# Moving delta*u*B of 14 of 16 states to GpSimd in the last image, with the scan tiled by one state

## The chip, the cores and the metric

The kernel runs on one core of one Trainium2 chip. The metric is the device time of one execution in microseconds (us). The kernel before was run three times: 26,690.43, 26,701.57 and 26,703.51 us, so the median is 26,701.57 us. One more execution was taken with the hardware profiler; all views below come from that one.

## The reference, cut to what matters

The input x holds 4 images of 128 x 128 positions with 128 channels, in fp32. Layer 0 is a group norm, a deformable 3x3 convolution (offsets, a bilinear gather, a depthwise and a pointwise convolution) and a residual sum. Layer 1 takes the result, norms it, and runs two Mamba blocks over it, each image row being one sequence of 128 steps. The part that the change touches is the selective scan of such a block:

```python
def _selective_scan(u, delta, A, Bm, Cm, Dp):
    deltaA = jnp.exp(jnp.einsum('btd,dn->btdn', delta, A))
    deltaBu = jnp.einsum('btd,btn->btdn', delta * u, Bm)
    ...
    def step(h, xs):
        dA, dBu, c = xs
        h = dA * h + dBu
        y = jnp.einsum('bdn,bn->bd', h, c)
        return (h, y)
    ...
    return y + u * Dp
```

There are d = 256 inner channels and n = 16 states. For each state the kernel needs the decay exp(delta*A), the product delta*u*B, the recurrence h = decay*h + product along the 128 steps, the product h*C, and the sum of that over the 16 states.

## The kernel before, in words

**Layer 0** goes image by image, through `layer0(b)`. Its costliest parts are `gather` (L364: GpSimd issues four indirect DMAs per half unit, 9,216 in all) and `sample` (L382: VectorE weights the gathered values, then TensorE sums and transposes them at L128 through `add_transposed`).

**Layer 1** goes by blocks of 4 rows (SR = 4), which is 512 positions (TB = 512) on the free axis, with channels on the 128 partitions, in two halves (NC = 2). There are 32 blocks per image and 128 in all. A job is one block through one of the two Mamba blocks, so there are 64 jobs per image and 256 in all. `pre(st, l)` makes u, the gate g, delta (tile `de`), delta*u (tile `du`), and a DRAM tile `bcd` with the rows of B and C. `main(st, l)` runs the scan in pairs of states (NQ = 2), 8 pairs per job, 2,048 pairs in all. For each pair:

- SyncE issues two DMAs that spread two rows of B (tile `bc0`) and two rows of C (tile `bc1`) over 128 partitions (L570), each with two buffers.
- ScalarE first writes zeros over the first step of each sequence in the decay tile `da` (L575), since the scan runs on through sequence after sequence and a decay of zero starts a new one. Then it writes the other 127 steps of the decays with four exponentials (L580). There are three `da` tiles of two states each.
- VectorE makes delta*u*B into `hs`, one instruction per state (L586). `hs` has one buffer of two states.
- VectorE scans both states in one instruction of 2,048 elements (L592). It writes over the decays in `da`.
- VectorE multiplies both states by C in one instruction, in place in `da` (L596).
- TensorE adds the transposed products into `y` in PSUM, 16 matmuls of 128x128 (L128).

L586 and L596 are written as `scalar_tensor_tensor` with `ones[:, 0:1]` as a scalar read from memory, where a plain `tensor_tensor` would compute the same.

```python
df = da.rearrange("p c n s t -> p (c n s t)")
nc.vector.tensor_tensor_scan(
    df, df, hs.rearrange("p c n t -> p (c n t)"), zero[:, 0:1], ALU.mult, ALU.add
)
```

After the last pair VectorE multiplies y by the gate (L607), TensorE transposes it and projects it; at the second Mamba block ScalarE copies the result to `ot` (L630), and SyncE writes it out (L632).

**What sets the order.** The two layers overlap by one image: the loop at the end of `block_kernel` steps through layer 0 of image b + 1 and layer 1 of image b in turn. So image 0's layer 0 runs alone, then three stretches have both, and layer 1 of the last image (image 3) runs alone. `pre` of the next job is written down ahead of `main` of the present one. Within this the framework's scheduler orders the instructions of each engine[...].

Of the kernel before, what the change touches and what calls it, by code (L numbers as in the profile page):

```python
# [10 lines left out]
F32 = mybir.dt.float32  # L11
I32 = mybir.dt.int32
AF = mybir.ActivationFunctionType
ALU = mybir.AluOpType
# [3 lines left out]
P = 128  # L18
G = 2
CG = 64  # L20
NT = 9
RB = 8
SR = 4
TB = SR * P
NGT = 4
NL = 2
NC = 2
NS = 16
NQ = 2
DTR = 8  # L30
DCONV = 4
# [32 lines left out]
def block_kernel(ctx: ExitStack, tc: tile.TileContext, a: dict, out: bass.AP):  # L64
    nc = tc.nc
    x = a["x"]
    B, H, W, C = x.shape
# [21 lines left out]
    cw = ctx.enter_context(tc.tile_pool(name="w", bufs=1))  # L89
# [4 lines left out]
    p2 = ctx.enter_context(tc.tile_pool(name="l1p2", bufs=1))  # L94
# [4 lines left out]
    def loadw(name, shape, src=None, pool=cw, tag=None):  # L99
        t = pool.tile(shape, F32, name=f"w_{name}", tag=tag) if tag else pool.tile(shape, F32, name=f"w_{name}")  # L100
        nc.sync.dma_start(t, a[name] if src is None else src)
        return t
# [13 lines left out]
    ones = cw.tile([P, P], F32, name="ones")  # L116
# [5 lines left out]
    inc = cw.tile([P, NL, DCONV, NC * P], F32, name="inc")  # L122
    aneg = cw.tile([P, NL, NC, NS], F32, name="aneg")
    ddiag = cw.tile([P, NL, NC, P], F32, name="ddiag")

    def add_transposed(o, v, start, stop):

        nc.tensor.matmul(o, v, ident, is_transpose=True, start=start, stop=stop, skip_group_check=True)  # L128
# [4 lines left out]


    dw = loadw("dw", [P, NT, NT], pool=p2, tag="dbl")
    dwb = loadw("dwb", [P, NT], pool=p2, tag="ot")
    pw = loadw("pw", [P, NT, CG], pool=p2, tag="u")
    pwb = loadw("pwb", [P, 1], pool=p2, tag="w1")
    nc.vector.tensor_tensor(
# [15 lines left out]
    alog = loadw("alog", [P, NL, NC, NS], pool=p2, tag="dbl")  # L155
    nc.scalar.activation(aneg, alog, AF.Exp)
    nc.vector.tensor_scalar(aneg, aneg, -1.0, None, ALU.mult)
    dpar = loadw("dpar", [P, NL, NC], pool=p2, tag="ot")
    for l in range(NL):
        for c in range(NC):  # L160
            nc.vector.tensor_scalar(ddiag[:, l, c, :], ident, dpar[:, l, c : c + 1], None, ALU.mult)
    inw = loadw("inw", [P, NL, NC * P], a["inw"][:, :, 0 : NC * P], pool=p2, tag="yg")
    cvw = loadw("cvw", [P, NL, DCONV, NC * P], pool=p2, tag="hs")
    for l in range(NL):
        nc.vector.tensor_tensor(
            inc[:, l], cvw[:, l], inw[:, l].unsqueeze(1).to_broadcast([P, DCONV, NC * P]), ALU.mult
        )


# [289 lines left out]

    NDA = 3
    das = [cw.tile([P, NC, NQ, SR, P], F32, name=f"da{i}") for i in range(NDA)]
    zero = cw.tile([P, NC * NQ * SR], F32, name="zero")
    nc.vector.memset(zero, 0.0)
    n_da = [0]

    NH = 2
# [5 lines left out]
    def next_h():  # L474
        n_h[0] += 1
        return hps[n_h[0] % NH]

    def load_x1(blk, nm):
        b, off = divmod(blk * TB, H * W)
        t = p2.tile([P, TB], F32, tag="x1t", name=f"x1t_{nm}", bufs=2)  # L480
        nc.sync.dma_start(t, x1[b][:, off : off + TB])
        return t
# [70 lines left out]
    def main(st, l):  # L553

        blk = st["blk"]
        nm = f"{blk}_{l}"

        y = psy.tile([P, SR, NC, P], F32, tag="y", name=f"y_{nm}")
        for i in range(SR):
            for c in range(NC):  # L560
                nc.tensor.matmul(  # L561
                    y[:, i, c], st["u"][:, c, i * P : (i + 1) * P], ddiag[:, l, c, :],
                    start=(i % 2 == 0 and c == 0), stop=False, skip_group_check=True,
                )
        for q in range(NS // NQ):
            bc = []
            for w in range(2):
                t = p2.tile([P, NQ, TB], F32, tag=f"bc{w}", name=f"bc{w}_{nm}_{q}", bufs=2)
                n0 = w * NS + q * NQ
                nc.sync.dma_start(t, st["bcd"][n0 : n0 + NQ, :].partition_broadcast(P))  # L570
                bc.append(t)
            da = das[n_da[0] % NDA]
            n_da[0] += 1

            nc.scalar.copy(da.rearrange("p c n s t -> p (c n s) t")[:, :, 0], zero)  # L575
            for c in range(NC):
                dv = st["delta"][:, c].rearrange("p (s t) -> p s t", s=SR)
                for n in range(NQ):
                    s = q * NQ + n
                    nc.scalar.activation(  # L580
                        da[:, c, n, :, 1:], dv[:, :, 1:], AF.Exp, scale=aneg[:, l, c, s : s + 1]
                    )
            hs = p2.tile([P, NC, NQ, TB], F32, tag="hs", name=f"hs_{nm}_{q}")

            for n in range(NQ):
                nc.vector.scalar_tensor_tensor(  # L586
                    hs[:, :, n, :], st["du"], ones[:, 0:1],
                    bc[0][:, n].unsqueeze(1).to_broadcast([P, NC, TB]),
                    op0=ALU.mult, op1=ALU.mult,
                )  # L590
            df = da.rearrange("p c n s t -> p (c n s t)")
            nc.vector.tensor_tensor_scan(  # L592
                df, df, hs.rearrange("p c n t -> p (c n t)"), zero[:, 0:1], ALU.mult, ALU.add
            )
            dc = da.rearrange("p c n s t -> p c (n s t)")
            nc.vector.scalar_tensor_tensor(  # L596
                dc, dc, ones[:, 0:1],
                bc[1].rearrange("p n t -> p (n t)").unsqueeze(1).to_broadcast([P, NC, NQ * TB]),
                op0=ALU.mult, op1=ALU.mult,
            )  # L600
            for c in range(NC):
                for n in range(NQ):
                    for i in range(SR):
                        add_transposed(y[:, i, c], da[:, c, n, i, :], False, q == NS // NQ - 1 and n == NQ - 1)
            yield
        gt = st["g"]
        nc.vector.tensor_tensor(gt, y.rearrange("p s c d -> p s (c d)"), gt, ALU.mult)  # L607
        yg = p2.tile([P, NC, TB], F32, tag="yg", name=f"yg_{nm}")
        for c in range(NC):
            pt = ps1.tile([P, SR, P], F32, tag="t", name=f"pyg_{nm}_{c}")  # L610
            for i in range(SR):
                nc.tensor.transpose(pt[:, i, :], gt[:, i, c * P : (c + 1) * P], ident)  # L612
            nc.scalar.copy(yg[:, c], pt.rearrange("p s t -> p (s t)"))
        po = ps1.tile([P, TB], F32, tag="t", name=f"pout_{nm}")
        if l < NL - 1:
            for c in range(NC):
                nc.tensor.matmul(po, ow[:, l, c, :], yg[:, c], start=(c == 0), stop=(c == NC - 1))
            st["h"] = next_h()
            nc.scalar.copy(st["h"][:, :, DCONV - 1 :], po.rearrange("p (s t) -> p s t", s=SR))
        else:  # L620
            x1t = load_x1(blk, f"o{nm}")
            for i in range(SR):
                o = po[:, i * P : (i + 1) * P]
                nc.tensor.matmul(o, x1t[:, i * P : (i + 1) * P], ident, start=True, stop=False)
                for c in range(NC):
                    nc.tensor.matmul(
                        o, yg[:, c, i * P : (i + 1) * P], ow[:, l, c, :], start=False, stop=(c == NC - 1)
                    )
            ot = p2.tile([P, SR, P], F32, tag="ot", name=f"ot_{nm}")
            nc.scalar.copy(ot.rearrange("p r c -> p (r c)"), po)  # L630
            b, row = divmod(blk * SR, H)
            nc.sync.dma_start(out[b, row : row + SR].rearrange("r w c -> w r c"), ot)  # L632
# [8 lines left out]
    def layer1():  # L641
        pre(*jobs[0])
        for i, job in enumerate(jobs):
            if i + 1 < len(jobs):
                pre(*jobs[i + 1])
            yield from main(*job)
# [11 lines left out]
    n0 = NJ * NT  # L658
# [67 lines left out]
def build(arrays):  # L726

    import concourse.bacc as bacc

    nc = bacc.Bacc("TRN2", target_bir_lowering=False, num_devices=1)  # L730
    a = {
        k: nc.dram_tensor(f"in_{k}", v.shape, mybir.dt.from_np(v.dtype), kind="ExternalInput").ap()
        for k, v in arrays.items()
    }
    out = nc.dram_tensor("out_0", arrays["x"].shape, F32, kind="ExternalOutput").ap()
    with tile.TileContext(nc) as tc:
        block_kernel(tc, a, out)
    return nc
# [9 lines left out]
```

## Time and profile before

| what | value |
|---|---|
| median of three runs | 26,701.57 us |
| the profiled execution's own time | 26,698.06 us |
| span of the profiled execution, first to last instruction | 26,696.0 us |
| VectorE (DVE) busy | 23,505.8 us, 88% |
| TensorE (PE) busy | 19,620.5 us, 73% |
| GpSimd (POOL) busy | 16,017.0 us, 60%; the last gather starts at 21,045.0 us |
| ScalarE (ACT) busy | 11,605.1 us, 43% |
| DMA | 143 GB/s on average |

The profile's first part gives the busy time of each engine. Its second part cuts the span into 40 equal slices of 667 us and gives the busy share of each slice in tenths, so a 9 is 90% or more. Its fifth part lists groups of like instructions with their count, their busy time, the mean duration of one in nanoseconds, and the idle time of the engine just before them, with what ended it. In a timeline a line is one instruction or a run of like ones: its start, its length, the engine, the line of the kernel, and what it writes and reads. Durations of neighbours on VectorE overlap a little (one starts some 0.08 us before the one ahead of it is over), so what an instruction costs is read from one start to the next.

### The profile page before, as it was taken

Reading aid. Unit: us, or ns where it says so; the run is one execution under the profiler, and the core shown is the slowest. Engines: PE = TensorE matmul, PEld = TensorE weight load, DVE = VectorE, ACT = ScalarE, POOL = GpSimd, SP = SyncE. Lnnn points to the kernel's source line nnn. Section 1 sums busy time; section 2 is a strip of 40 time slices with the busy share of each in tenths; the row PEclk is TensorE's granted clock in tenths of the full one; section 3 lists DMA queues with packets and bytes.
Section 4 is the critical chain, followed back from the end, with each engine's and each line's share of the span. In section 5 each row is a group of like instructions: output and inputs, shape, how many; then the busy total and the mean of one; then the engine's idle time right before and its main releaser. Section 6 shows DMA issues by size and latency. Waiting matters only on the chain. (4 is left out here: it accounts for less than half of the span.)

```text
span 26696.0 us, 294801 instructions
## 1 busy us (share of the span) xinstructions
PE 19620.5 (73%) x112196; PEld 13523.4 (51%) x112196; DVE 23505.8 (88%) x14042; ACT 11605.1 (43%) x18181; POOL 16017.0 (60%) x9222
## 2 busy tenths in 40 slices
PE   4777788878888778887888778888888655555555
PEld 3444455555555555555555555555555443434344
DVE  2232289999999999999999999999999999999999
ACT  0000044444444544444444454444445455555554
POOL 4777777878877767888878667877878400000000
PEclk7888888888999888888998888899998866666666
DMA  5363344456544444455544444444444333333332
GB/s 146 114 172 107 106 147 155 157 170 183 165 153 154 149 144 155 158 173 181 164 154 153 148 143 151 156 150 152 154 154 156 130 107 106 107 106 107 107 106 102
DMA packets 1994602, 3804.53 MB, mean 143 GB/s; under 512 B 771796, under 2 KB 1116116, under 8 KB 1993053
## 3 DMA queue, kind: packets, MB, share of 16 engines
q1 hardware_dynamic: 1550812, 2577.13, 29.9%
q0 software_dynamic: 442368, 1208.55, 14.4%
q8 instruction: 880, 14.42, 0.2%
q14 instruction: 542, 4.43, 0.0%
HBM read 3567.63 MB, written 217.05 MB: 142 GB/s over the span
## 5 line engine op out<-in xcount | busy, mean ns | idle before, releaser
L364 POOL DMA_INDIRECT gt<-table,idx x9216 | 16016.3, 1738 | 5031.5 <-issue 2999.5
L592 DVE TENSOR_TENSOR_SCAN da<-da,zero,hs 128x2048 f32<-128x2048 f32 x2048 | 9176.1, 4481 | 351.7 <-ACT da L580 247.1
L128 PE MATMUL y<-ident,da 128*128 128x128 f32 x32768 | 5252.0, 326 | 3956.1 <-DVE da L596 3955.4
L580 ACT ACTIVATE da<-de,aneg 128x508 f32<-128x508 f32 x8192 | 5550.5, 712 | 5605.2 <-PE y L128 5351.0
L128 PEld LDWEIGHTS y<-ident,da 128*128 128x128 f32 x32768 | 4682.4, 171 | 4953.3 <-DVE da L596 2520.6
L415 PE MATMUL acc<-s,wc 128*64 128x256 f32 (+3 forms) x38400 | 6403.2, 453 | 761.4 <-ACT s L396 760.9
L586 DVE SCALAR_TENSOR_TENSOR hs<-du,ones,bc 128x1024 f32<-128x1024 f32 x4096 | 5093.2, 1277 | 0.0
L415 PEld LDWEIGHTS acc<-s,wc 128*64 128x64 f32 x38400 | 3352.0, 145 | 3083.2 <-issue 1446.2
L596 DVE SCALAR_TENSOR_TENSOR da<-da,ones,bc 128x2048 f32<-128x2048 f32 x2048 | 4807.9, 2348 | 25.9
L382 DVE TENSOR_TENSOR gw<-gt,wt 128x1024 f32<-128x1024 f32 x2304 | 2786.4, 1213 | 2133.3 <-DMA gt<-table,idx 1500.9
L128 PE MATMUL p<-ident,gw 128*128 128x128 f32 x18432 | 2724.3, 299 | 1714.1 <-DVE gw L382 1706.7
L128 PEld LDWEIGHTS p<-ident,gw 128*128 128x128 f32 x18432 | 2292.8, 154 | 2329.3 <-DVE gw L382 1752.7
L396 ACT COPY s<-p 128x512 f32<-128x512 f32 x1152 | 668.6, 581 | 3989.8 <-PE p L128 3982.0
L501 PE MATMUL pu<-hp,inc 128*128 128x512 f32 x4096 | 1808.3, 593 | 0.0
L580 ACT ACT_TABLE_LOAD x1016 | 1303.5, 1283 | 16.8 <-PE y L128 5.7
L501 PEld LDWEIGHTS pu<-hp,inc 128*128 128x128 f32 x4096 | 751.2, 188 | 865.9 <-issue 865.2
L508 ACT ACTIVATE u<-pu,w_cvb 128x512 f32<-128x512 f32 x512 | 324.6, 684 | 1468.9 <-PE y L561 1461.4
L561 PEld LDWEIGHTS y<-ddiag,u 128*128 128x128 f32 x4096 | 579.5, 200 | 192.0 <-issue 192.0
L612 PE MATMUL pyg<-ident,g 128*128 128x128 f32 x2048 | 353.9, 328 | 425.7 <-DVE g L607 424.8
L546 ACT ACT_TABLE_LOAD x500 | 641.5, 1283 | 8.9
L561 PE MATMUL y<-ddiag,u 128*128 128x128 f32 x4096 | 612.1, 284 | 0.0
L263 PE MATMUL pof<-xn,w_offw 128*64 128x512 f32 x2304 | 585.0, 613 | 20.0 <-ACT xn L257 12.0
(118 smaller groups left out, 11036.3 us busy)
## 6 DMA issues: line engine op xcount, KB each, us to landing
bc<-bcd SPq DMA_DIRECT2D x4096, 512.0 KB
gt<-table,idx POOLq DMA_INDIRECT x9216
table<-xt SPq DMA_DIRECT2D x984, 128.0 KB
xt<-in_x SPq DMA_DIRECT2D x124, 320.0 KB
xr<-in_x SPq DMA_DIRECT2D x128, 256.0 KB
x<-xo SPq DMA_DIRECT2D x128, 256.0 KB
x1t<-x SPq DMA_DIRECT2D x128, 256.0 KB
x1t_o<-x SPq DMA_DIRECT2D x128, 256.0 KB
```

What stands on the lines that cost most here:

```text
L128: nc.tensor.matmul(o, v, ident, is_transpose=True, start=start, stop=stop, skip_group_check=True)
L364: nc.gpsimd.indirect_dma_start(out=gt[:, v, r], out_offset=None, in_=flat, in_offset=bass.IndirectOffsetOnAxis(ap=idx[:, ri, o : o + 1], a ...
L382: nc.vector.tensor_tensor(gw.rearrange("p r s v c -> p (r s) v c"), gts[h].rearrange("p v r (s c) -> p (r s) v c", c=CG), wv.unsqueeze(3). ...
L396: nc.scalar.copy(st[:, :, 1 : W + 1], p4)
L415: nc.tensor.matmul(accs[b, j + i0][CG * g : CG * g + CG, q : q + rb - ra, :], wc[sl, v, e, :], st[p + 4 * g if p < 4 else 8][sl, ra:rb, kx ...
L501: nc.tensor.matmul(px.rearrange("p (s t) -> p s t", s=SR), inc[:, l, j, c * P : (c + 1) * P], h[:, :, j : j + P], start=(j == 0), stop=(j ...
L546: nc.scalar.activation(du[:, c], w1, AF.Ln)
L561: nc.tensor.matmul(y[:, i, c], st["u"][:, c, i * P : (i + 1) * P], ddiag[:, l, c, :], start=(i % 2 == 0 and c == 0), stop=False, skip_grou ...
L580: nc.scalar.activation(da[:, c, n, :, 1:], dv[:, :, 1:], AF.Exp, scale=aneg[:, l, c, s : s + 1])
L586: nc.vector.scalar_tensor_tensor(hs[:, :, n, :], st["du"], ones[:, 0:1], bc[0][:, n].unsqueeze(1).to_broadcast([P, NC, TB]), op0=ALU.mult, ...
L592: nc.vector.tensor_tensor_scan(df, df, hs.rearrange("p c n t -> p (c n t)"), zero[:, 0:1], ALU.mult, ALU.add)
L596: nc.vector.scalar_tensor_tensor(dc, dc, ones[:, 0:1], bc[1].rearrange("p n t -> p (n t)").unsqueeze(1).to_broadcast([P, NC, NQ * TB]), op ...
```

## The change

In every image, the unit of the scan becomes one state in place of two.

- `da` becomes four tiles of one state each. They are set to zero once, and the exponentials never write the first step of a sequence, so the zeros stay. The zeroing copy at L575 goes. That works because the scan no longer writes into `da`: it writes over its other input, `hs`, and takes 0.0 as its first value in place of a scalar in memory.
- `hs` becomes a tile of one state with five buffers. The product with C is made in place there, one instruction per state, and TensorE transposes from `hs`.
- B is loaded by state (tile `bs`, three buffers, one row per DMA), C by pairs as before (tile `cs`, two buffers).
- Where the block belongs to the last image, delta*u*B of all states but 7 and 15 is made by GpSimd as a `tensor_tensor`. There, VectorE's own products (states 7 and 15, and all products with C) are plain `tensor_tensor` too. In the other images they stay `scalar_tensor_tensor`.
- To make room, `ot` shares the one buffer of `w1`, the convolution weights `cvw` are loaded in two halves, and two small weights use other tags.

```diff
-    NDA = 3
-    das = [cw.tile([P, NC, NQ, SR, P], F32, name=f"da{i}") for i in range(NDA)]
-    zero = cw.tile([P, NC * NQ * SR], F32, name="zero")
-    nc.vector.memset(zero, 0.0)
+    NDA = 4
+    das = [cw.tile([P, NC, SR, P], F32, name=f"da{i}") for i in range(NDA)]
+    for t in das:
+        nc.vector.memset(t, 0.0)
...
+        last = blk * SR // H == B - 1
+        on_pool = set(range(NS)) - {7, 15} if last else set()
...
-        for q in range(NS // NQ):
-            bc = []
-            for w in range(2):
-                t = p2.tile([P, NQ, TB], F32, tag=f"bc{w}", name=f"bc{w}_{nm}_{q}", bufs=2)
-                n0 = w * NS + q * NQ
-                nc.sync.dma_start(t, st["bcd"][n0 : n0 + NQ, :].partition_broadcast(P))
-                bc.append(t)
+        for n in range(NS):
+
+            bs = p2.tile([P, TB], F32, tag="bs", name=f"bs_{nm}_{n}", bufs=3)
+            nc.sync.dma_start(bs, st["bcd"][n : n + 1, :].partition_broadcast(P))
+            if n % NQ == 0:
+                cs = p2.tile([P, NQ, TB], F32, tag="cs", name=f"cs_{nm}_{n}", bufs=2)
+                nc.sync.dma_start(cs, st["bcd"][NS + n : NS + n + NQ, :].partition_broadcast(P))
             da = das[n_da[0] % NDA]
             n_da[0] += 1
-
-            nc.scalar.copy(da.rearrange("p c n s t -> p (c n s) t")[:, :, 0], zero)
             for c in range(NC):
                 dv = st["delta"][:, c].rearrange("p (s t) -> p s t", s=SR)
...
+                nc.scalar.activation(da[:, c, :, 1:], dv[:, :, 1:], AF.Exp, scale=aneg[:, l, c, n : n + 1])
+
+
+            hs = p2.tile([P, NC, TB], F32, tag="hs", name=f"hs_{nm}_{n}", bufs=5)
+            bv = bs.unsqueeze(1).to_broadcast([P, NC, TB])
+            cv = cs[:, n % NQ].unsqueeze(1).to_broadcast([P, NC, TB])
+            if n in on_pool:
+                nc.gpsimd.tensor_tensor(hs, st["du"], bv, ALU.mult)
+            elif last:
+                nc.vector.tensor_tensor(hs, st["du"], bv, ALU.mult)
+            else:
+                nc.vector.scalar_tensor_tensor(hs, st["du"], ones[:, 0:1], bv, op0=ALU.mult, op1=ALU.mult)
+            hf = hs.rearrange("p c t -> p (c t)")
             nc.vector.tensor_tensor_scan(
-                df, df, hs.rearrange("p c n t -> p (c n t)"), zero[:, 0:1], ALU.mult, ALU.add
+                hf, da.rearrange("p c s t -> p (c s t)"), hf, 0.0, ALU.mult, ALU.add
             )
...
+            if last:
+                nc.vector.tensor_tensor(hs, hs, cv, ALU.mult)
+            else:
+                nc.vector.scalar_tensor_tensor(hs, hs, ones[:, 0:1], cv, op0=ALU.mult, op1=ALU.mult)
             for c in range(NC):
...
+                for i in range(SR):
+                    add_transposed(y[:, i, c], hs[:, c, i * P : (i + 1) * P], False, n == NS - 1)
...
-            ot = p2.tile([P, SR, P], F32, tag="ot", name=f"ot_{nm}")
+            ot = p2.tile([P, SR, P], F32, tag="w1", name=f"ot_{nm}")
```

More of the change, by code (lines that the diff above doesn't have):

```diff
@@ L135, in block_kernel @@
     dw = loadw("dw", [P, NT, NT], pool=p2, tag="dbl")
-    dwb = loadw("dwb", [P, NT], pool=p2, tag="ot")
+    dwb = loadw("dwb", [P, NT], pool=p2, tag="yg")
     pw = loadw("pw", [P, NT, CG], pool=p2, tag="u")
@@ L157, in block_kernel @@
     nc.vector.tensor_scalar(aneg, aneg, -1.0, None, ALU.mult)
-    dpar = loadw("dpar", [P, NL, NC], pool=p2, tag="ot")
+    dpar = loadw("dpar", [P, NL, NC], pool=p2, tag="u")
     for l in range(NL):
@@ L162, in block_kernel @@
     inw = loadw("inw", [P, NL, NC * P], a["inw"][:, :, 0 : NC * P], pool=p2, tag="yg")
-    cvw = loadw("cvw", [P, NL, DCONV, NC * P], pool=p2, tag="hs")
     for l in range(NL):
+        cvw = p2.tile([P, DCONV, NC * P], F32, tag="hs", name=f"w_cvw_{l}", bufs=5)
+        nc.sync.dma_start(cvw, a["cvw"][:, l])
         nc.vector.tensor_tensor(
-            inc[:, l], cvw[:, l], inw[:, l].unsqueeze(1).to_broadcast([P, DCONV, NC * P]), ALU.mult
+            inc[:, l], cvw, inw[:, l].unsqueeze(1).to_broadcast([P, DCONV, NC * P]), ALU.mult
         )
@@ L572, in main @@
             da = das[n_da[0] % NDA]
             n_da[0] += 1
-            nc.scalar.copy(da.rearrange("p c n s t -> p (c n s) t")[:, :, 0], zero)
             for c in range(NC):
                 dv = st["delta"][:, c].rearrange("p (s t) -> p s t", s=SR)
[L578 to L591, printed above, removed]
+                nc.scalar.activation(da[:, c, :, 1:], dv[:, :, 1:], AF.Exp, scale=aneg[:, l, c, n : n + 1])
+            hs = p2.tile([P, NC, TB], F32, tag="hs", name=f"hs_{nm}_{n}", bufs=5)
@@ L592, in main @@
             nc.vector.tensor_tensor_scan(
-                df, df, hs.rearrange("p c n t -> p (c n t)"), zero[:, 0:1], ALU.mult, ALU.add
+                hf, da.rearrange("p c s t -> p (c s t)"), hf, 0.0, ALU.mult, ALU.add
             )
[L595 to L600, printed above, removed]
+            if last:
+                nc.vector.tensor_tensor(hs, hs, cv, ALU.mult)
+            else:
+                nc.vector.scalar_tensor_tensor(hs, hs, ones[:, 0:1], cv, op0=ALU.mult, op1=ALU.mult)
@@ L601, in main @@
             for c in range(NC):
[L602 to L605, printed above, removed]
+                for i in range(SR):
+                    add_transposed(y[:, i, c], hs[:, c, i * P : (i + 1) * P], False, n == NS - 1)
+            if n % NQ == NQ - 1:
+                yield
         gt = st["g"]
```

## The prediction

> **What bounds the kernel now.** I read the slices of the span first, then the sums by stretch, then the groups by line, then VectorE's timeline in one job.
>
> ```profile
> PE 19620.5 (73%) x112196; PEld 13523.4 (51%) x112196; DVE 23505.8 (88%) x14042; ACT 11605.1 (43%) x18181; POOL 16017.0 (60%) x9222
> DVE  2232289999999999999999999999999999999999
> POOL 4777777878877767888878667877878400000000
> ```
>
> The first five slices are layer 0 of image 0 alone. From then on DVE is full. POOL stops at about 21,050 us: behind that lies the last image's layer 1, alone. The sums by stretch (busy time and instructions of PE, PEld, DVE, ACT, POOL, then clock and DMA) give the two stages that the change touches:
>
> ```profile
> 3400.00:21400.00 18000.00, 14369.69 (x84305) 9887.87 (x84300) 17529.80 (x10448) 8701.47 (x13705) 13633.95 (x6925) 0.89 0.48 156
> 21400.00:26696.00 5296.00, 2762.14 (x12528) 2119.47 (x12528) 5018.22 (x2467) 2662.11 (x4051) 0.00 (x0) 0.69 0.31 106
> ```
>
> DVE is busy 97% of the **middle stage** (17,530 of 18,000) and 95% of the **last** (5,018 of 5,296). ACT and PE are busy 48% and 80% of the middle, 50% and 52% of the last. So both stages are priced in DVE time. Three groups of DVE carry it:
>
> ```profile
> L592 DVE TENSOR_TENSOR_SCAN da<-da,zero,hs 128x2048 f32<-128x2048 f32 x2048 | 9176.1, 4481 | 351.7 <-ACT da L580 247.1
> L586 DVE SCALAR_TENSOR_TENSOR hs<-du,ones,bc 128x1024 f32<-128x1024 f32 x4096 | 5093.2, 1277 | 0.0
> L596 DVE SCALAR_TENSOR_TENSOR da<-da,ones,bc 128x2048 f32<-128x2048 f32 x2048 | 4807.9, 2348 | 25.9
> ```
>
> Neighbours overlap, so I price by starts, from DVE's timeline in the last stage:
>
> ```profile
> 24061.74 1.28 DVE L586 SCALAR_TENSOR_TENSOR hs<-du,ones,bc 128x1024 f32<-128x1024 f32 x1
> 24062.94 0.68 DVE L548 SCALAR_TENSOR_TENSOR de<-pdt,e 128x512 f32<-128x512 f32 x1
> 24063.54 1.28 DVE L586 SCALAR_TENSOR_TENSOR hs<-du,ones,bc 128x1024 f32<-128x1024 f32 x1
> 24064.73 1.22 DVE L549 TENSOR_TENSOR de<-de,du 128x1024 f32<-128x1024 f32 x1
> 24065.87 4.48 DVE L592 TENSOR_TENSOR_SCAN da<-da,zero,hs 128x2048 f32<-128x2048 f32 x1
> 24070.26 1.20 DVE L550 TENSOR_TENSOR du<-de,u 128x1024 f32<-128x1024 f32 x1
> 24071.38 2.35 DVE L596 SCALAR_TENSOR_TENSOR da<-da,ones,bc 128x2048 f32<-128x2048 f32 x1
> 24073.64 2.48 DVE L586 SCALAR_TENSOR_TENSOR hs<-du,ones,bc 128x1024 f32<-128x1024 f32 x2
> 24076.25 4.48 DVE L592 TENSOR_TENSOR_SCAN da<-da,zero,hs 128x2048 f32<-128x2048 f32 x1
> 24080.77 2.35 DVE L596 SCALAR_TENSOR_TENSOR da<-da,ones,bc 128x2048 f32<-128x2048 f32 x1
> ```
>
> Start to start: a product with the pointer scalar costs 1.20 us at 1,024 elements and 2.26 at 2,048, so 1.06 per 1,024 and 0.14 fixed. A plain product costs 1.13, fixed 0.07. The one without a pointer, L548, costs 0.60 at 512, fixed 0.07 too: the pointer costs 0.07. The scan costs 4.39. Where neighbours depend on each other there is a stall: products to scan 2.61 in place of 2.40 (0.21), scan to its product with C 4.52 in place of 4.39 (0.13).
>
> [...] These are a scan and the next instructions of DVE, and POOL's gathers over the same time:
>
> ```profile
> 12006.85 4.47 DVE L592 TENSOR_TENSOR_SCAN da<-da,zero,hs 128x2048 f32<-128x2048 f32 x1
> 12011.25 0.80 DVE L216 TENSOR_TENSOR xt<-xt,row_b 128x640 f32<-128x640 f32 x1
> 12011.96 2.34 DVE L596 SCALAR_TENSOR_TENSOR da<-da,ones,bc 128x2048 f32<-128x2048 f32 x1
> ```
> ```profile
> 12004.92 0.95 POOL L364 DMA_INDIRECT gt<-table,idx  x1 [0.30 <-issue]
> 12008.06 4.03 POOL L364 DMA_INDIRECT gt<-table,idx  x1 [0.31 <-issue]
> 12012.39 2.74 POOL L364 DMA_INDIRECT gt<-table,idx  x1 [0.30 <-DVE xt L216]
> ```
>
> A free gather takes 0.95 us. The one at 12,008.06 begins in the scan and ends at 12,012.09, 0.77 after the scan's end (12,011.32). The next begins in the product L596 and ends at 12,015.13, 0.83 after that. So a gather, which reads an index, does not get past a scan or a product of two SBUF tensors. The other direction, DVE held by a long POOL instruction, no row shows, for POOL has none.
>
> [...]
>
> [...] 4.39 us for 2,048 elements is twice 2.13 and 0.13.
>
> **The change, part by part.**
>
> *Middle stage, 1,536 pairs of states.* A pair costs 2 x 1.20 + 4.39 + 2.26 = 9.05 us of DVE now, without stalls. Afterwards it takes two products with B, two scans, two products with C: 4 x 1.20 plus two scans. A scan of 1,024 elements is half of 4.26 and a fixed part: 0.07 if 0.0 in the instruction saves the pointer's 0.07, else 0.13; 2.20 to 2.26. I take 2.20, as L548 shows the saving on another instruction. The pair becomes 9.20: +0.15, or 1,536 x 0.15 = +230 us. With 2.26 it is +0.27, +415.
>
> *Stalls.* Two dependent neighbours per pair become four. In the middle stage layer 0's instructions lie between them most times already (L216 above, behind the scan). With five buffers of `hs`, the next state's product can go between a scan and its product with C, which one buffer forbade. If all stalls go, today's at most 0.34 a pair go (-520 us, more than the 470 us of all DVE idle time there); if none of the new ones is covered, +520. I take -80, since most are already covered. Middle: **+150**, ends about -250 and +650.
>
> *Last stage.* It starts near 21,350 us and lasts 5,345: 83.5 us for each of 64 jobs. By rows: 8 pairs x (9.05 + 0.34) = 75.1; the rest of a job on DVE (L547, L548 twice each at 0.60, L549, L550, L607 at 1.13) 5.8; the remaining 2.6 are waits for decays. Afterwards, of a POOL state DVE has a scan and a plain product, 2.20 + 1.13 = 3.33 us[...]. Both of DVE's are of the kind that the gathers can't get past, and POOL's reads two SBUF tensors throughout. So I add them[...]. The two DVE states cost 2 x 1.13 + 2.20 = 4.46. [...] POOL can work while DVE waits for decays or reads PSUM (L548, L607: 2.3 a job), which hides up to some 5 us; the handing over, 28 times a job, isn't priced by any row: at 0 to 0.2 us each it costs 0 to 5.6. I set these two against each other with half a microsecond left: 93.3, +9.8 a job, 64 x 9.8 = **+630**. [...] If POOL hides beside DVE after all, the sum is in the first rival.
>
> *Edits at nothing.* The zeroing copy (2,048 x 209 ns on ACT) goes: 430 us of an engine that is busy half the time. The exponentials of a state wait for the scan four states before in place of TensorE's transposes; the lead is three states, 14 us, where before it was one to two pairs; without it DVE's 247 us of waits on L580 grow. Matmuls stay the same in number. The loads move the same bytes in 24 issues a job in place of 16; SyncE spends 0.32 us on each, 8 us of 83. A row of B is asked for two states ahead (9 us), behind the queue's waits for C's buffers; before, DVE waited on none of these loads; if one lands late, DVE or POOL waits for the rest. On POOL's queue nothing else stands. `ot` in the buffer of `w1`: the job's next L545 comes 20 us after the write-out is issued. The first stage has DVE idle; memsets and loads hide there.
>
> **Sum.** 26,696 + 150 + 630 = 27,476 for the span; with the 2 us that the execution lies above its span and the median's 3.5 above that, **27,480 us**.
>
> **Rivals.**
> 1. *POOL works beside DVE.* [...] DVE's job of 14 x 3.33 + 2 x 4.46 + 5.8 = 61.3, with 4 of waits for decays 65. That is -18.2 a job, -1,165 in all; with the middle's +150, 1,015 below today's median: about **25,690**. For it: DVE's instructions last no longer while gathers run. Against: [...] it is plainly held back.
> 2. *Partly hidden.* [...] At 1.4 us hidden it is 0.53 x 896 = 475 us below today's median: **26,230**.
> 3. *Stalls in the middle too:* the scheduler keeps the order as written, hence +650 in place of +150: **27,980**.
>
> **How the numbers follow.** Serial, as forecast: 0.53. Rival 3: 0.15. Rival 1: 0.14. Rival 2 beyond break-even: 0.13. About break-even: 0.05. A measurement of this kernel tells some 0.2% from no change, so faster 0.27, same 0.05, slower 0.68. The likeliest case's own range is 26,900 to 28,150. With both signs the range of 8 in 10 reaches from 26,000, leaving rival 1 out, to 28,150.
>
> **What would show it.** [...] In the middle stage: scans near 2.28 us by their own length, and hs products between a scan and its product. I am wrong if POOL's reads and DVE's second input don't exclude each other over a whole instruction.

## The result, and the profile after

| | before | after |
|---|---|---|
| median of the runs, four each | 26,696.0 us | 27,157.9 us |
| span of the profiled execution | 26,696.0 | 27,155.8 |
| layer 0 of image 0 alone, up to the first scan | 3,471 | 3,461 |
| middle stage, first scan to the last image's first scan | 17,880 | 17,793 |
| last stage, the last image's layer 1 | 5,345 | 5,902 |

The ratio is 1.0179, with a 95% interval from 1.0167 to 1.0191: the change made the kernel slower. The forecast had +784 us in all; it was +462. The stages are cut at the scans' starts in the timeline. The last stage lost 557 us; the middle one, where the forecast had a loss of 150, gained 87.

The page of the kernel after, its sums and its slices:

```profile
PE 19519.0 (72%) x112196; PEld 13523.5 (50%) x112196; DVE 24157.6 (89%) x17245; ACT 11156.8 (41%) x15975; POOL 17239.8 (63%) x10118
DVE  2232299999999999999999999999999999999999
POOL 3777766677766466777767466766676345454454
```

POOL now has work to the end. DVE is as full as before, but with what? The groups of DVE in the last stage of the kernel after (busy time, mean length of one in ns, idle time ahead of it):

```profile
L594 DVE TENSOR_TENSOR_SCAN hs<-da,hs 128x1024 f32<-128x1024 f32 x1007 | 2786.0, 2796 | 302.9 <-POOL hs L588 302.9
L598 DVE TENSOR_TENSOR hs<-hs,cs 128x1024 f32<-128x1024 f32 x1008 | 2033.2, 2041 | 2.2
L590 DVE TENSOR_TENSOR hs<-du,bs 128x1024 f32<-128x1024 f32 x126 | 284.5, 2258 | 0.0
L548 DVE SCALAR_TENSOR_TENSOR e<-w,e 128x512 f32<-128x512 f32 x126 | 216.4, 1717 | 0.0
L549 DVE SCALAR_TENSOR_TENSOR de<-pdt,e 128x512 f32<-128x512 f32 x126 | 85.5, 679 | 0.0
```

A plain product of 1,024 elements took 1.21 us before and takes 2.04 on average here. L548 (two inputs in SBUF) went from 0.67 to 1.72 us; before it was L547:

```profile
L547 DVE SCALAR_TENSOR_TENSOR e<-w,e 128x512 f32<-128x512 f32 x124 | 83.6, 674 | 0.0
```

L549 reads one of its inputs from PSUM (`pdt`, which TensorE writes), and it kept its 0.68. In the timeline of the kernel after, DVE first, then POOL, the lengths come in steps:

```profile
24012.37 3.30 DVE L590 TENSOR_TENSOR hs<-du,bs 128x1024 f32<-128x1024 f32 x1
...
24018.88 4.46 DVE L594 TENSOR_TENSOR_SCAN hs<-da,hs 128x1024 f32<-128x1024 f32 x2
24023.26 4.44 DVE L598 TENSOR_TENSOR hs<-hs,cs 128x1024 f32<-128x1024 f32 x2
```
```profile
24011.22 3.38 POOL L588 TENSOR_TENSOR hs<-du,bs 128x1024 f32<-128x1024 f32 x1 [5.37 <-PE y L128]
...
24021.06 4.42 POOL L588 TENSOR_TENSOR hs<-du,bs 128x1024 f32<-128x1024 f32 x1 [3.19 <-PE y L128]
```

The POOL product at 24,021.06 starts beside the second of two scans, which is over at 24,023.34, and ends 2.14 us after that. The two products of DVE that follow take 4.44 us where two take 2.33: 2.11 more, just the time that POOL was at work. So each waits out the other, like two users of one door. Of the 896 POOL products of the last stage, 768 begin in a DVE instruction with two inputs in SBUF: 646 end 2.13 to 2.24 us after it, the other 122 let one more pass and end 4.31 to 4.33 us after the first. The other way round, all 434 products with C that begin in a POOL product end 1.08 or 1.09 us after it.

In the middle stage the sums by stretch (PE, PEld, DVE, ACT, POOL), before and after, show DVE busier by 134 us and idle for 221 us less (422 to 201):

```profile
3471.00:21351.00 17880.00, 14276.24 (x83817) 9827.60 (x83816) 17457.93 (x10387) 8645.38 (x13623) 13581.66 (x6875) 0.89 0.48 156
```
```profile
3461.00:21254.00 17793.00, 14106.79 (x83824) 9894.34 (x83822) 17592.05 (x13458) 8302.13 (x11931) 11885.02 (x6882) 0.88 0.51 157
```

### The profile page after: what moved, and what is told of

It is laid out like the page before. It is cut to its first block, busy times and chain, and to the rows that moved or that the text cites. A ratio compares the mean times of both kernels' runs of the same rounds, so it can differ in the third digit from the quotient of the medians.

```text
span 27155.8 us, 300272 instructions
## 1 busy us (share of the span) xinstructions
PE 19519.0 (72%) x112196; PEld 13523.5 (50%) x112196; DVE 24157.6 (89%) x17245; ACT 11156.8 (41%) x15975; POOL 17239.8 (63%) x10118
## 4 chain that ended last, share of the span: by engine, by line
issue 35%; POOL 29%; DVE 26%; PE 5%; DMA 3%; ACT 2%; SPq 1%; DVEq 0%; POOLq 0%; ACTq 0%
POOL gt L365 28%; DVE hs L594 9%; DVE hs L592 3%; DVE hs L598 3%; DVE hs L600 3%; DMA gt<-table,idx 3%; DVE gw L383 2%; POOL hs L588 1%; DVE e L548 1%; PE pdb L522 1%; PE y L128 1%; PE acc L416 1%; DVE hs L590 1%; ACT da L581 1%; DVE de L550 1%
## 5 line engine op out<-in xcount | busy, mean ns | idle before, releaser
L365 POOL DMA_INDIRECT gt<-table,idx x9216 | 14289.3, 1550 | 6661.4 <-DVE gw L383 3514.8
L594 DVE TENSOR_TENSOR_SCAN hs<-da,hs 128x1024 f32<-128x1024 f32 x4096 | 9754.0, 2407 | 315.8 <-POOL hs L588 309.3
L128 PE MATMUL y<-ident,hs 128*128 128x128 f32 x32768 | 5378.9, 328 | 5073.3 <-DVE hs L598 2847.3
L581 ACT ACTIVATE da<-de,aneg 128x508 f32<-128x508 f32 x8192 | 5486.1, 711 | 8108.6 <-DVE hs L594 8066.6
L128 PEld LDWEIGHTS y<-ident,hs 128*128 128x128 f32 x32768 | 4663.3, 171 | 6167.7 <-DVE hs L598 3068.2
L588 POOL TENSOR_TENSOR hs<-du,bs 128x1024 f32<-128x1024 f32 x896 | 2949.9, 3304 | 3223.7 <-PE y L128 2821.2
L592 DVE SCALAR_TENSOR_TENSOR hs<-du,ones,bs 128x1024 f32<-128x1024 f32 x3072 | 3856.1, 1283 | 26.9 <-PE y L128 25.3
L600 DVE SCALAR_TENSOR_TENSOR hs<-hs,ones,cs 128x1024 f32<-128x1024 f32 x3072 | 3844.6, 1274 | 2.2
L598 DVE TENSOR_TENSOR hs<-hs,cs 128x1024 f32<-128x1024 f32 x1024 | 2062.6, 2038 | 2.2
L514 PE MATMUL pr<-w_resw,hp 128*128 128x256 f32 x2048 | 574.0, 430 | 247.6 <-ACT u L509 247.4
L522 PE MATMUL pdb<-u,w_xpw 128*41 128x512 f32 x1024 | 614.7, 732 | 20.0 <-ACT g L519 18.6
```

Source lines behind the costliest of these rows:

```text
L365: nc.gpsimd.indirect_dma_start(out=gt[:, v, r], out_offset=None, in_=flat, in_offset=bass.IndirectOffsetOnAxis(ap=idx[:, ri, o : o + 1], a ...
L522: nc.tensor.matmul(pdb[0:XP], xpw[:, l, c, :], u[:, c], start=(c == 0), stop=(c == NC - 1))
L581: nc.scalar.activation(da[:, c, :, 1:], dv[:, :, 1:], AF.Exp, scale=aneg[:, l, c, n : n + 1])
L588: nc.gpsimd.tensor_tensor(hs, st["du"], bv, ALU.mult)
L592: nc.vector.scalar_tensor_tensor(hs, st["du"], ones[:, 0:1], bv, op0=ALU.mult, op1=ALU.mult)
L594: nc.vector.tensor_tensor_scan(hf, da.rearrange("p c s t -> p (c s t)"), hf, 0.0, ALU.mult, ALU.add)
```

## The experiments

All change the kernel after. All but the one with seven states also take the products off GpSimd in the last image, by the edit of the first run, which is not shown again. The first run and those with seven states, with unread products and with fills ran where layer 0 alone took some 3,470 us, as above. The others ran on chips where it took 4,084 to 4,172 us, for a reason that no run here shows; the kernel before had a median of 27,329 to 27,396 us there. So those are compared by stages, and their base is the kernel without GpSimd, run once more there. Groups of a last stage are taken from 21,300 to 26,200 us, most of it.

**No product on GpSimd.**

```diff
-        on_pool = set(range(NS)) - {7, 15} if last else set()
+        on_pool = set()
```

> The changed kernel with no product on GpSimd: in the last image VectorE makes all 16, as plain products; the tiling by one state stays. Theory [...]: a job of the last image is 16 x (2.20 + 2 x 1.13) + 5.8 = 77.2 us of VectorE and some 2.6 of waits, 64 x 79.8 = 5,110 in place of 5,902: 26,370 us in all (26,250 to 26,450), so faster than the kernel before. Rival (it is the tiling by one state that costs in the last image, through shorter instructions, stalls and a shorter lead of the decays): the last image stays above 5,700, 27,000 or more in all.

Measured: 26,296 us, ratio to the kernel before 0.9851 (0.9835 to 0.9868). The last stage took 5,029 us, the middle 17,782. That is in the range of the theory, that GpSimd's products and VectorE's instructions go one after the other. So the rest of the change is a gain of 1.5% over the kernel before, and the products on GpSimd lose all of it and some 460 us more: 5,901.5 - 5,029.3 = 872 us. The rival, that the tiling costs, falls. DVE's lengths are back:

```profile
L594 DVE TENSOR_TENSOR_SCAN hs<-da,hs 128x1024 f32<-128x1024 f32 x999 | 2258.0, 2278 | 0.0
L598 DVE TENSOR_TENSOR hs<-hs,cs 128x1024 f32<-128x1024 f32 x999 | 1196.3, 1213 | 2.1
L590 DVE TENSOR_TENSOR hs<-du,bs 128x1024 f32<-128x1024 f32 x999 | 1187.5, 1209 | 0.0
```

This kernel once more, beside later ones:

> The changed kernel with no product on GpSimd once more, as the base for the two kernels beside it: the first three images' layer 1 in 17,780 us, the last in 5,030, and layer 0 alone ahead of them as long as this core takes for it (3,470 or 4,160).

Measured: 17,793 and 5,029 us, after 4,127 of layer 0 alone. The stages repeat within 0.1%. This is the base of all that follows but the runs with seven states, with unread products and with fills, whose base is the first run.

**Seven states on GpSimd in place of 14.**

```diff
-        on_pool = set(range(NS)) - {7, 15} if last else set()
+        on_pool = set(range(1, NS, 2)) - {15} if last else set()
```

> GpSimd makes 7 of 16 states (1, 3, 5, 7, 9, 11, 13) in the last image, every second one, in place of 14. Theory [...]: half of the difference between no state and 14, so about 26,370 + 395 = 26,760 us. Rival (what costs is a wait once a job, when GpSimd begins late on a new job's first states): a wait per job doesn't halve, 27,000 us or more. Second rival (with VectorE products between them GpSimd's hide): 26,400 or below.

Measured: 26,600 us, the last stage 5,332: 303 us over none, where 14 states cost 872. The first seven cost 0.68 us each (303 / 448), the next seven 1.27. The cost grows with the number, but not by halves: neither the number of the theory, that each product costs the same (26,760), nor a rival's came. The difference lies in DVE's idle time: 92 us of the last stage with no product on GpSimd, 38 with seven, 324 with 14, where DVE waited some 300 us for GpSimd's results (the first group above); with seven it waited for none. What the products add to DVE's busy time is alike: with 1.13 us for each product that DVE no longer makes, 1.93 us a product with seven and 1.84 with 14.

**GpSimd's products made, but read by nobody.**

```diff
+            if last and n not in (7, 15):
+                nc.gpsimd.tensor_tensor(spare, st["du"], st["delta"], ALU.mult)
```

> VectorE makes all 16 products of the last image, and GpSimd makes 14 more products of the same size a job (delta*u times delta) into a tile that nobody reads: work is added, the output stays. Nobody waits for GpSimd. Theory [...]: 896 products hold VectorE for about 2.1 us each, 1,880, less what falls into VectorE's own waits and its instructions from PSUM, some 200 to 300: 28,000 us (27,800 to 28,250). Rival (the loss came from waiting for GpSimd's results): as without GpSimd, about 26,370.

(`spare` is a part of `wc`, weights of layer 0 that the last stage doesn't need.)

Measured: 28,255 us, just above the range that I gave. The last stage took 6,965, so 1,936 us for 896 products or **2.16 us each**. No engine waits for these results, so the rival, a wait for results, can't be what makes a product dear. I had also expected 200 to 300 us to hide in DVE's waits; in the trace none of POOL's time lies beside idle time of DVE. In the groups of its last stage DVE's product with C is again too long, and so is the scan:

```profile
L597 DVE TENSOR_TENSOR_SCAN hs<-da,hs 128x1024 f32<-128x1024 f32 x717 | 2060.8, 2892 | 0.0
L601 DVE TENSOR_TENSOR hs<-hs,cs 128x1024 f32<-128x1024 f32 x717 | 1346.4, 1893 | 1.6
```

**GpSimd fills, and reads nothing.**

```diff
+            if last and n not in (7, 15):
+                nc.gpsimd.memset(spare, 1.0)
+                nc.gpsimd.memset(spare, 2.0)
```

> As the run with unread products, but GpSimd fills the unread tile twice with a constant in place of each product: two instructions of 1,024 elements that write and read nothing. Theory [...]: as without GpSimd, about 26,370, and VectorE's instructions keep their lengths. Rival (any GpSimd instruction that uses SBUF holds VectorE, writing too): 1,792 fills of a microsecond or so each, 27,300 or more.

Measured: 26,307 us, the last stage 5,029, to the microsecond that without GpSimd, although POOL was at work for some 1,700 us of it (1,792 x 952 ns). The groups of its last stage, DVE's and POOL's:

```profile
L602 DVE TENSOR_TENSOR hs<-hs,cs 128x1024 f32<-128x1024 f32 x998 | 1194.6, 1212 | 2.1
```
```profile
L596 POOL MEMSET wc<- 128x1024 f32 x733 | 698.1, 952 | 42.1
L595 POOL MEMSET wc<- 128x1024 f32 x732 | 697.2, 952 | 42.1
```

1,792 fills beside DVE cost nothing: DVE's products with C keep their 1,212 ns (1,213 without GpSimd), so it isn't GpSimd's writing. That leaves its reading, which the next run tests with one input.

**GpSimd copies: one input.**

```diff
+            if last and n not in (7, 15):
+                nc.gpsimd.tensor_copy(spare, st["du"])
```

> VectorE makes all products; GpSimd makes 14 copies of delta*u a job into a tile that nobody reads: one tensor read, one written, 1,024 elements. Theory (any GpSimd instruction that reads SBUF keeps VectorE out for its own length): a copy lasts about as long as a fill, 0.95 us, so 896 x 0.95 = 850 us less 100 to 200 that fall into VectorE's waits: the last image in 5,700 us (5,600 to 5,900). Rival (it takes two inputs on GpSimd to get in VectorE's way): 5,030 to 5,100.

Measured: the last stage took 5,730 us, 701 over none, 0.78 us for each copy, in the theory's range. One input on GpSimd is enough. POOL's copies are at least 1.91 us long by the trace, but that is not their work alone. In time, DVE and POOL in turn:

```profile
25007.44 1.98 DVE L601 TENSOR_TENSOR hs<-hs,cs 128x1024 f32<-128x1024 f32 x1
25008.42 1.91 POOL L595 COPY wc<-du 128x1024 f32<-128x1024 f32 x1
25009.35 2.05 DVE L601 TENSOR_TENSOR hs<-hs,cs 128x1024 f32<-128x1024 f32 x1
25010.39 1.92 POOL L595 COPY wc<-du 128x1024 f32<-128x1024 f32 x1
```

The first copy begins in a DVE product that is over at 25,009.42, and ends 0.91 us after that. The next DVE product ends 1.07 us after this copy, and the next copy 0.91 us after that product. So each waits for the whole of the other. All 896 copies begin in a DVE instruction; 864 of them end 0.83 to 0.90 us after it, the other 32 let two more pass first. So a copy's own work is at most some 0.9 us, as the theory had it, and it keeps DVE out for about that long: a product beside it takes 2.05 us in place of 1.21.

**The last image's products with the memory scalar.** Of the change only the tiling is left, with what belongs to it: five buffers of `hs`, zeros kept in `da`, 0.0 as the scan's first value.

```diff
-            elif last:
-                nc.vector.tensor_tensor(hs, st["du"], bv, ALU.mult)
...
-            if last:
-                nc.vector.tensor_tensor(hs, hs, cv, ALU.mult)
-            else:
+            if True:
                 nc.vector.scalar_tensor_tensor(hs, hs, ones[:, 0:1], cv, op0=ALU.mult, op1=ALU.mult)
```

> No product on GpSimd, and the last image's products written with the scalar from memory again, as in the other images: of the whole change only the tiling is left. Theory (the memory scalar costs 0.065 us an instruction, whether anything is gathered or not): 2,048 products cost 135 us more than in the run without GpSimd (26,296): 26,430 us. Rival (plain products bring nothing by themselves; the last image's gain is the tiling's): 26,300.

Measured: middle 17,794 us, last 5,120, 90 over the base. The products are some 1,295 ns long in place of 1,211 there. DVE's busy time rose by 118 us, and its idle time fell by 27, since the base waits more for ScalarE (L548: 78 us there, 50 here). So plain products bring 90 us of the 135 expected, and the tiling with its parts 5,345 - 5,120 = 225.

**The scan's first value from memory.**

```diff
+    zero = cw.tile([P, 1], F32, name="zero")
+    nc.vector.memset(zero, 0.0)
...
-                hf, da.rearrange("p c s t -> p (c s t)"), hf, 0.0, ALU.mult, ALU.add
+                hf, da.rearrange("p c s t -> p (c s t)"), hf, zero, ALU.mult, ALU.add
```

> No product on GpSimd, and the scan takes its first value from memory again (a zero in a tile) in place of 0.0 in the instruction. Theory (the prediction's lower price of a scan, 2.20 us, came from this): 4,096 scans by 0.065 us, +265: 26,560 us. Rival (the first value costs the same either way): 26,300.

Measured: middle 17,999 us, 205 over the base; last 5,036, 7 over it. The scans took 2,347 ns in place of 2,272 in the middle, and DVE's busy time there rose by 210 us: about the 200 expected for 3,072 scans. In the last stage 67 us were expected and only 7 came: DVE's busy time rose by 57 us, and its idle time fell by 50, most of it in waits of L548 for ScalarE (78 us in the base, 29 here).

**Plain products in all images.**

```diff
-            elif last:
+            elif True:
...
-            if last:
+            if True:
```

> No product on GpSimd, and plain products in all images. Theory (with the shorter scans GpSimd's gathers have time to spare, so the window that the memory scalar leaves them isn't needed any more): 6,144 products by 0.065 us, -400 us at most, 25,900 to 26,100 us. Rival (a gather then waits out every VectorE instruction that it meets, comes late, and VectorE waits for it): 26,300 or more, with gathers of over 2 us on average.

Measured: ratio to the kernel before 1.0024 (1.0012 to 1.0035). The middle stage took 18,346 us, 553 over the base. My theory falls and the rival holds. The group of gathers in the middle stage of the base, then of this kernel, and DVE's wait for them in this one (the base has none):

```profile
L365 POOL DMA_INDIRECT gt<-table,idx x6878 | 11859.6, 1724 | 5635.7 <-DVE gw L383 3528.1 <-issue 1864.5 <-DVE loc L289 114.3
```
```profile
L365 POOL DMA_INDIRECT gt<-table,idx x6878 | 15107.4, 2196 | 2960.2 <-issue 1975.4 <-DVE gw L383 878.2 <-DMA gt<-table,idx 39.9
DVE gw L383 <- DMA gt<-table,idx: 846.0, 221, 7.4
```

DVE is busy for 374 us less, as the plain products promise, but idle for 927 more. GpSimd's spare time (5,636 us idle) was no cushion. Two gathers that begin at the start of a product show why, in the base beside a product with the memory scalar (the second of the two), here beside a plain one:

```profile
12058.73 2.47 DVE L592 SCALAR_TENSOR_TENSOR hs<-du,ones,bs 128x1024 f32<-128x1024 f32 x2
12059.93 0.95 POOL L365 DMA_INDIRECT gt<-table,idx  x1 [0.30 <-issue]
```
```profile
12132.30 1.22 DVE L590 TENSOR_TENSOR hs<-du,bs 128x1024 f32<-128x1024 f32 x1
12132.37 1.97 POOL L365 DMA_INDIRECT gt<-table,idx  x1 [0.30 <-DMA gt<-table,idx]
```

The first gather takes its free 0.95 us and is over before the product; the second ends 0.82 us behind the product. Counted over the middle stage, of the gathers that begin in the first 0.1 us of a product with B, 1,429 of 1,446 run free in the base, and 5 of 629 here. One that begins later doesn't: of the 551 in the middle stage of the kernel after, where the code is the base's, none ends before the product, and the first ends 0.81 us behind it. So the memory scalar leaves a gather a window at the start of the instruction.

**Two and three buffers of hs.**

```diff
-            hs = p2.tile([P, NC, TB], F32, tag="hs", name=f"hs_{nm}_{n}", bufs=5)
+            hs = p2.tile([P, NC, TB], F32, tag="hs", name=f"hs_{nm}_{n}", bufs=2)
```

(The convolution weights `cvw`, which use the same buffers once at the start, get as many.)

> No product on GpSimd, and two buffers of hs in place of five. Theory (spare buffers let the scheduler put other states' instructions between a product, its scan and the product with C, so that no stall is left): the stalls come back, up to 0.34 us a state in the last image (350 us, so 5,380) and some 0.1 in the others (300, so 18,080). Rival (the other images gained by something else, such as gathers that get through sooner between shorter instructions): 5,030 to 5,100 and 17,780 to 17,850.

Measured: middle 19,912 us, last 5,845; far more than stalls can cost, so this run doesn't price them. It brought a new wait, of a product for the transposes that still read the buffer (middle stage, then last):

```profile
DVE hs L592 <- PE y L128: 1375.3, 742, 13.9
DVE hs L590 <- PE y L128: 840.7, 223, 10.0
```

> No product on GpSimd, three buffers of hs. Two buffers brought a new wait, of a product for TensorE's transposes out of the same buffer. Theory (that wait takes 2.7 us of transposes per state, which one more buffer covers, and a third state's product can still go between): the last image within 100 us of five buffers, 5,030 to 5,130, the others 17,790 to 17,950. Rival (all five buffers are needed): 5,300 or more in the last image.

Measured: middle 18,778, last 5,460. The theory falls, and the rival's number came; the wait is still there (549 us in the middle, 392 of the 431 lost in the last stage). For the transposes of a state the theory had 2.7 us; eight at the 326 ns that one takes on average before make 2.6. So the tiling by one state needs more than three buffers; four wasn't tried.

**A state's three instructions in a row.** This run asks for the stalls alone, with five buffers.

```diff
+            if n > 0:
+                tc.add_manual_dep(
+                    ins.ins, cprod.ins.name,
+                    mybir.DependencyInfo(mybir.DependencyClass.NoSync, mybir.DependencyReason.DATA),
+                    reason="order",
+                )
```

(`ins` is a state's product with B, `cprod` the product with C of the state before.)

> No product on GpSimd, five buffers of hs, but each state's product is ordered behind the product with C of the state before, so that a state's three VectorE instructions stand one behind the other, as written. Theory (the spare buffers' worth is that other states' instructions fill the stalls of dependent neighbours): 0.21 + 0.13 = 0.34 us a state in the last image, less what other instructions fill, so 5,029 + 300 = 5,330 us (5,280 to 5,400) there; in the other images a quarter or so uncovered, 17,790 + 260 = 18,050 (17,950 to 18,200). Rival (the lower idle time after the change is from the shorter scans alone, which let gathers and decays come sooner): 5,030 to 5,100 and 17,780 to 17,850.

Measured: middle 18,342 us, 549 over the base; last 5,201, 172 over it. Both are off the rival's numbers, but also outside the theory's ranges, the middle above and the last below. The timeline of the last stage of this kernel, then of the base:

```profile
26004.05 1.22 DVE L590 TENSOR_TENSOR hs<-du,bs 128x1024 f32<-128x1024 f32 x1
26005.37 2.29 DVE L600 TENSOR_TENSOR_SCAN hs<-da,hs 128x1024 f32<-128x1024 f32 x1
26007.70 1.23 DVE L604 TENSOR_TENSOR hs<-hs,cs 128x1024 f32<-128x1024 f32 x1
26008.84 1.22 DVE L590 TENSOR_TENSOR hs<-du,bs 128x1024 f32<-128x1024 f32 x1
```
```profile
24021.21 4.47 DVE L594 TENSOR_TENSOR_SCAN hs<-da,hs 128x1024 f32<-128x1024 f32 x2
24025.59 2.34 DVE L598 TENSOR_TENSOR hs<-hs,cs 128x1024 f32<-128x1024 f32 x2
24027.84 2.36 DVE L590 TENSOR_TENSOR hs<-du,bs 128x1024 f32<-128x1024 f32 x2
24030.11 4.47 DVE L594 TENSOR_TENSOR_SCAN hs<-da,hs 128x1024 f32<-128x1024 f32 x2
```

In a row, product to scan takes 1.32 us and scan to product 2.33: 4.79 a state. In the base the scheduler does two states at a time, scan, scan, product, product: 8.90 for two, 4.45 a state, so nothing stands straight behind what it depends on. Added up from the starts, the stalls of dependent neighbours are some 230 us of the last stage here and 7 in the base; the 172 are less because waits of L548 fell from 78 us to 10. In the middle the stalls are 336 us in place of 19, and longer waits (idle gaps of over 0.15 us) 370 in place of 192, of which 142 are for gathers. So the stalls are the larger part of the 549, and not all of it.

## Why the prediction was right, and where its sizes were off

The forecast was +784 us and the change cost 462. Of the 322 between, 237 belong to the middle stage and 73 to the last.

**Adding the two times, right.** The step that decided the sign was to add GpSimd's product to DVE's time. The trace of before showed one half of the ground for it, gathers held back by DVE. The other half, DVE held by POOL, and the time of a product on POOL were the author's assumptions: no row of before showed them. Both are measured now. The unread products cost DVE 2.16 us each, and the shortest product takes 2.35 on POOL. The forecast had a job of the last stage at 93.3 us; it took 5,902 / 64 = 92.2. Since an unread product costs 2.16 us, a fill nothing and a copy 0.78, it is the reading, whatever waits for the result. By the test that the prediction set at its end it was right: on both sides an instruction waits for the whole of the other (646 of 768 POOL products behind one instruction and 122 behind two, all 434 products with C).

The sum of the last stage closes: the base's 5,029, less 896 x 1.13 = 1,012 of products that left DVE, is 4,017. DVE's longer instructions add (from the groups after and base) 1,008 x 0.83 + 1,007 x 0.52 + 126 x 1.05 + 126 x 1.03 = 1,622, and the wait for POOL 303: 5,942. The base's 78 us of waits for ScalarE are gone after: 5,864 against 5,902 measured. So some 0.35 us of each POOL product (2.16 - 1,622 / 896) did hide; in the trace 153 us of POOL's time lie beside idle time of DVE, and 118 beside its instructions that read PSUM. That those don't hold POOL shows before too: all 170 gathers of its middle stage that begin in L548 or L607 take 0.94 to 0.96 us.

The prediction set what hides (up to 5 us a job) against the handing over (0 to 5.6, the author's estimate) and left half a microsecond. They did cancel, 4.9 us a job against a wait of 4.7, but by luck: the wait isn't a price of each handover, as that step had it. DVE waits for POOL 63 times, once at each turn of a job, 4.9 us at a time on average, when POOL makes the next job's first products late.

**The middle stage, wrong in what it left out.** The forecast had +150: +230 for instructions and -80 for stalls. Measured was -87. Stalls can be counted in the traces, from starts. Before, 414 of 1,536 scans stand straight behind their products, and 404 products with C behind their scan; so most were covered, as the step put it, and the stalls came to 125 us. After they come to 19: **-106**. Longer waits, idle gaps of over 0.15 us, went from 363 to 189: **-174**. That leaves **+193** for the instructions. It is 37 less than forecast, as a product with C behind another one starts 1.18 us after it, not 1.20, and a scan ahead of another state's product with C takes 2.18. So both terms of the forecast held, and what failed is that the waits were put at nothing. Most of their fall is DVE's wait for gathers, of which next to nothing is left after. Before, and then the gathers before and after:

```profile
DVE gw L382 <- DMA gt<-table,idx: 112.1, 49, 4.2
```
```profile
L364 POOL DMA_INDIRECT gt<-table,idx x6875 | 13581.7, 1976 | 3996.7 <-issue 1990.5 <-DVE gw L382 1912.7 <-DVE loc L288 46.5
L365 POOL DMA_INDIRECT gt<-table,idx x6878 | 11874.9, 1727 | 5616.4 <-DVE gw L383 3509.1 <-issue 1862.3 <-DVE loc L289 114.4
```

All 1,329 gathers of the middle stage before that begin later than 0.1 us into a scan end 0.75 to 0.77 us after the scan, and so do all 1,128 after; the scan is half as long now (2,277 ns in place of 4,481), and these gathers take 2.00 us on average in place of 4.16. That this is why gathers as a whole are shorter is argued from the trace, not tested apart. The prediction's reading that a gather doesn't get past a scan or a product is too wide as well: the free gather that it shows, at 12,004.92, runs inside a product (L586) from its start. So do 1,243 of the 1,255 gathers of the middle stage before that begin in the first 0.1 us of an L586.

**The other steps.** The price of the scan was right, 2.20 us from start to start, and so was 0.07 for its memory scalar. In the last image the tiling brings 225 us, mostly in stalls and waits that go, and plain products 90. The forecast carried this inside its sum for the job but did not set it apart, so that it did not see that the change without GpSimd is a gain. Of the edits at nothing, none shows up among DVE's waits: no wait for L581, none for loads of B or C; POOL waited for loads of B, 106 us of the last stage. Rival 1 is excluded, rival 3 came out with the other sign, and rival 2's break-even, (630 + 150) / 896 = 0.87 us of each product hidden beside DVE, was not reached (0.35).

The best version of all that ran is the change without GpSimd, at 26,296 us.

## What to carry to other kernels

Before moving work from VectorE to GpSimd, look at what VectorE does meanwhile. Here GpSimd read SBUF and VectorE's instructions had two inputs there, and the two times added: a product that left VectorE saved 1.13 us, and one that GpSimd made unread cost 2.16. What lay beside VectorE's idle time (153 us of the last stage) or its reads of PSUM (118 us) was all that the trace shows as hidden. In such a case add the times first, and ask then what hides. A change of several parts wants one run with the suspect part out: here it turned a loss of 1.8% into a gain of 1.5%. Splitting a chain of dependent instructions into smaller units wants buffers enough to interleave two units: here five sufficed, and three lost 985 us in the middle stage.

## What the runs showed that was not expected

- A GpSimd copy of 1,024 elements keeps VectorE out for some 0.85 us; a fill of as many, 0.95 us long, not at all. A copy that waits for VectorE looks twice as long in the trace, 1.91 us where its own work is at most some 0.9: its length there includes the wait for the other engine.
- A scalar read from memory costs VectorE about 0.07 us an instruction (scans of 2,347 ns in place of 2,272), and in the products it is worth more than that beside gathers: without it there the gathers' mean went from 1,724 to 2,196 ns and the stage lost 553 us. With it in the scans too, the mean fell to 1,433 ns, and of the gathers that begin in the first 0.1 us of a scan 881 of 893 run free, where 22 of 1,158 do in the base. But there was no wait for gathers left to save, and the stage lost 205 us. Why the scalar leaves this window, these runs do not show.
